# Two graph layers on one core: how the list matrices are compared, how the largest entries are taken, and where the last packing and the ranking stand

## The chip, the cores and the metric

The kernel runs on one core of one Trainium2 chip. The metric is the device time of one execution in microseconds (us), as the median over runs. The profile is one further execution, recorded by the hardware profiler; its times are counted from the start of its span. TensorE is PE in the profile, VectorE is DVE, ScalarE is ACT, GpSimd is POOL and SyncE, which issues plain DMAs, is SP.

## The reference

There are N = 2708 nodes with D = 512 features and a sparse matrix `adj` of 2708 x 2708 with about eight entries besides the diagonal in a row. Two layers follow each other, each with a residual and a layer norm:

```
# layer 0
d  = rowsum(adj) ** -0.5
x1 = layernorm(x + relu((d[:,None] * adj * d[None,:]) @ x @ W + b))
# layer 1, H = 4 heads
z     = x1 @ W_node + b_node
feats = z @ K[h]                               # per head
attn  = softmax(s_i + NEG * (1 - adj))         # NEG = -1e10
out   = layernorm(x1 + relu(mean_h(attn @ feats)))
```

With NEG = -1e10 the softmax of a row puts all its weight on the row's largest entry of `adj`, as long as the second is far enough below it. So layer 1 is computed as `u = x1 @ M + c`, with M and c made from `W_node`, `b_node` and the mean of `K`, and each node then takes the row of `u` that its largest entry points at. Rows where two entries are too near set a value in `bad`; if any is set, a dense version of the whole runs behind the fast one.

## The kernel before

Rows are worked in 21 full blocks of 128 (`ib` 0 to 20) and a last one of 20 rows, 22 blocks in all (`NB`), in an order written out by hand: nothing is reordered by a scheduler, each engine has its own queue, and a queue runs in program order.

**Setup stage, to about 139 us.** Each block of `adj` is loaded (1354 KB), the diagonal is taken out by POOL, ACT sums the rows (L299), and `v = d * (x @ W)` goes to memory as `v_d`. DVE searches each block in three column ranges: eight largest values and their places, `vals` and `ats` (L318, L319). The searches of the last blocks run on into the main stage, two or three for each block.

**Main stage, 139 to about 428 us.** A block's product with the sparse matrix is a sum of nine chunks (`CHUNKS`, c = 0 to 8). In each third of the columns one chunk ("d") takes every row's first entry, and two ("l") take the other entries as a list of 128 slots each. For every chunk POOL issues an indirect DMA that gathers 128 rows of `v_d` (L611, one per chunk, nine per block). PE multiplies the gathered rows by a small matrix `s` (L672), or DVE scales and adds them for some "d" chunks (L662). The order is by chunk: in chunk n = 9 * ib + c the program first issues the gathers up to chunk n + 11 (later up to n + 22, by two more for each block), so POOL's queue holds gathers that lie ahead of what PE consumes.

The lists are made by `hot` (DVE, L392 and L393: a matrix with a one for each pair of slot and row), `enlist` (PE, L402: this matrix times the packed entries of the block) and `listed` (DVE, L414 to L439). `hot` of block ib + 3 stands at chunk 5 of block ib, `enlist` four chunks later, `listed` six. `pack_1`, `pack_2`, `pack_3` bring the search's results into the packed form, for the blocks in `GROUPS` 0-3, 4-11 and 12-21; the last group is packed when the search has ended.

At the end of a block DVE adds the block's own row (`own_term`, L698 or L700; bias by PE where `bias_on_pe`), takes relu and residual (`norm_1`, L711, L712), ACT squares (L727 or L721), and the inverse root comes from POOL (L733, in `norm_2`, up to block 9) or from ACT and DVE (`root_1`, `root_2`). ACT writes the norm (`norm_3`, L756), PE turns it at chunk 7 of the next block (L224), and `u_product` (L235) makes `u` of a block one block later, at chunk 5. PE waits in its queue for each of these.

**The rank steps.** Some rows (more than eight entries in a third, or lists over 256; and the 20 rows of the last block) can't be done by lists. They are marked in `flag`, counted and collected as one extra block of up to 128 rows, called L. `largest` finds each row's largest entry among its three thirds and its diagonal; `rank_1`, `rank_1b`, `rank_2` count and number the marked rows and those whose largest entry points at a late block; `rank_3` builds one-hot matrices (`l_hot`, L923); `rank_3b` multiplies on PE; `rank_4` turns the sheet into row numbers. Then `listed_a` makes POOL gather the 128 marked rows of `adj` itself (`l_a`, L983) and of x (`l_x`). ACT sums `l_a` (`listed_sum`, L989), POOL takes its root (`listed_root`), and PE multiplies `l_a` by all of v: 22 times `listed_turn` (a transposition, L1003) and `listed_product` (L1012), fed by loads `l_v` on SP. After the last one `listed_norm` (L1019) finishes block L.

The places of these steps are in `plan`, whose keys are (blocks after the search ended, chunk). The search ends in block 7, so `found_at` is 8 and (0, 5) is chunk 5 of block 8. `listed_turn` runs at the odd chunks from chunk 4 of block 11 on, `listed_product` at the even ones, two behind.

**Last stage.** Once `u` of the first 18 blocks and of block L is in memory, POOL gathers for every node the row of `u` that it needs (L1052), DVE and ACT finish the second norm, and the results are stored; rows that were marked are scattered by indirect DMAs (L1029).

Of the kernel before, what the change touches and what calls it, by code (L numbers as in the profile page):

```python
# [47 lines left out]
P = 128  # L48
# [15 lines left out]
def tile_two_graph_layers(  # L64
# [60 lines left out]
    nc.gpsimd.memset(half_neg, -0.5)  # L125
    ones = const.tile([P, 1], F32, name="ones")
# [66 lines left out]
    nc.gpsimd.iota(own_row, pattern=[[P, NB]], base=0, channel_multiplier=1, **small_numbers)  # L193
    for t in range(T):
        nc.gpsimd.memset(third[:, t, :], float(CUT[t]))
# [50 lines left out]
    def pieces(dst, left):  # L246

        piece = wpool.tile([T, D], BF16, name="piece_3", bufs=1)
        for k in range(T):
            nc.vector.tensor_copy(piece, left)  # L250
            if k == 0:
                nc.vector.tensor_scalar(dst, piece, ident[:T, 0:1], None, op0=ALU.mult)
            else:
                nc.vector.scalar_tensor_tensor(dst, piece, ident[:T, k : k + 1], dst, op0=ALU.mult, op1=ALU.add)
            if k < T - 1:
                nc.vector.tensor_sub(left, left, piece)
# [128 lines left out]
    def hot(ib):  # L385

        lo = max(g for g in GROUPS if g <= ib)
        ends = starts[lo]
        h_t = search.tile([P, T, 2 * P], BF16, name="hot", bufs=2)
        for t in range(T):  # L390
            past = search.tile([P, 2 * P], BF16, name="past", bufs=2)
            nc.vector.tensor_scalar(past, slots, ends[:, 1, ib - lo, t : t + 1], None, op0=ALU.is_gt)  # L392
            nc.vector.scalar_tensor_tensor(  # L393
                h_t[:, t, :], slots, ends[:, 0, ib - lo, t : t + 1], past, op0=ALU.is_gt, op1=ALU.subtract
            )
        hots[ib] = h_t

    def enlist(ib):
        ls = sheets[ib] = p_one.tile([P, D], F32, name="ls")
        h_t = hots.pop(ib)  # L400
        for k in range(NL):
            nc.tensor.matmul(  # L402
                ls[:, k * W_REC : (k + 1) * W_REC],
                h_t[:, k // 2, k % 2 * P : (k % 2 + 1) * P],
                packed[:, ib, k // 2, :],
                start=True,
                stop=True,
            )

    def listed(ib):  # L410
# [5 lines left out]
        nc.vector.tensor_copy(minus_row, ls[:, :, 0])  # L416
# [36 lines left out]
    def group(lo):  # L453
# [4 lines left out]
        if hi == NB:  # L458
            nc.vector.memset(flag[: N - full, NS:], 1.0)
# [228 lines left out]
    def bias_on_pe(ib):  # L688

        return ib < 9  # L690

    def own_term(ib):
# [3 lines left out]
        if bias_on_pe(ib):  # L696
            if ib in BY_VECTOR:
                nc.vector.tensor_scalar(vs[:pr], vs[:pr], self_d[:pr, ib : ib + 1], None, op0=ALU.mult)  # L698
# [122 lines left out]
    def largest():  # L821

        best, nxt, sel, lower, dif = (col() for _ in range(5))
        j = dl["j"] = search.tile([P, NB], F32, name="largest")
        nc.vector.tensor_copy(best, vals[:, :, 0, 0])
        nc.vector.tensor_copy(nxt, vals[:, :, 0, 1])
        nc.vector.tensor_copy(j, cols[:, :, 0, 0])
        for t in range(1, T + 1):
            other = vals[:, :, t, 0] if t < T else aii
            at_t = cols[:, :, t, 0] if t < T else own_row  # L830
            nc.vector.tensor_tensor(sel, other, best, op=ALU.is_gt)
            nc.vector.tensor_tensor(lower, other, best, op=ALU.min)
            nc.vector.tensor_max(nxt, nxt, lower)
            if t < T:
                nc.vector.tensor_max(nxt, nxt, vals[:, :, t, 1])
            nc.vector.tensor_max(best, best, other)
            nc.vector.tensor_tensor(dif, at_t, j, op=ALU.subtract)
            nc.vector.tensor_mul(dif, dif, sel)
            nc.vector.tensor_add(j, j, dif)
        nc.vector.tensor_copy(idx, j)  # L840
        nc.vector.tensor_scalar(best, best, 1.0, -NEG, op0=ALU.subtract, op1=ALU.mult)
# [605 lines left out]
```

## Time and profile before

| | |
|---|---|
| Median of 14 runs | 489.35 us (486.18 to 491.05) |
| Profiled execution | 488.0 us, its span 486.3 us |
| Instructions in the span | 5318 |
| PE busy | 374.9 us, 1129 matmuls |
| DVE busy | 391.9 us, 1079 instructions |
| ACT busy | 312.5 us |
| POOL busy | 307.3 us |
| Mean granted PE clock | 0.92 |
| DMA traffic | 140.67 MB, mean 289 GB/s |

The profiled execution's own time is 1.7 us above its span and 1.35 us below the median of the runs. A block's end is the end of its L712 on DVE: block 7 ends at 252.3 us, block 8 at 271.3, block 9 at 284.8, block 10 at 298.2, block 11 at 314.0, block 12 at 326.1, block 16 at 378.7 and block 20 at 428.0 us. A busy PE is not PE at its peak, since ends of matmuls are modelled; the distance from one start to the next is the better measure.

### The profile page before, as it was taken

The numbers are of one execution on the slowest core, as the hardware profiler recorded it, in microseconds if no ns is written. First come the engines' busy times: TensorE is split into PE (matmuls) and PEld (weight loads), VectorE is DVE, ScalarE is ACT, GpSimd is POOL, SyncE is SP. The second block draws the span as 40 slices with busy tenths as digits, with TensorE's granted clock in tenths as the row PEclk, the third lists the DMA queues.
The fourth block names the chain that finished last, engine by engine and source line by source line (L and its number), as shares of the span: only waits on it lengthen the run. The fifth ranks groups of instructions, "written<-read, shape, count | busy, mean of one in ns | idle before, by whom it ended". The sixth has DMA issues, their size and how long they took to land.

```text
span 486.3 us, 5318 instructions
## 1 busy us (share of the span) xinstructions
PE 374.9 (77%) x1129; PEld 167.9 (35%) x1129; DVE 391.9 (81%) x1079; ACT 312.5 (64%) x575; POOL 307.3 (63%) x434
## 2 busy tenths in 40 slices
PE   4978787687987989799979859699999999870000
PEld 3434343333223333343433324344444344340000
DVE  2899989889699999999999997676666797567661
ACT  1599999897985556776773453865566322348780
POOL 2343544454477677777877677777777665677713
PEclk9999999898998989899998959899999999996555
DMA  7999999999538678889889789999999788468962
GB/s 223 423 394 415 425 341 373 350 339 350 195 113 292 190 235 265 268 249 310 271 259 297 225 264 358 388 335 387 356 363 316 231 272 269 126 191 293 326 212 84
DMA packets 51565, 140.67 MB, mean 289 GB/s; under 512 B 10617, under 2 KB 10617, under 8 KB 48688
## 3 DMA queue, kind: packets, MB, share of 16 engines
q0 software_dynamic: 21840, 68.29, 45.3%
q1 hardware_dynamic: 29684, 71.95, 39.3%
q14 instruction: 30, 0.25, 0.2%
q8 instruction: 11, 0.18, 0.2%
HBM read 117.33 MB, written 24.99 MB: 293 GB/s over the span
## 4 chain that ended last, share of the span: by engine, by line
DVE 31%; DMA 29%; PE 21%; issue 8%; POOL 5%; ACT 4%; SPq 1%; POOLq 0%; DVEq 0%; ACTq 0%
DMA a<-in_adj_dram 18%; PE acc L672 8%; DVE ats L319 6%; PE po L235 6%; DVE vals L318 5%; PE acc_l L1012 4%; DMA g<-u_e,idx 3%; DVE hot L393 3%; DMA x<-in_x_dram 3%; DVE vs L662 2%; DMA l_a<-in_adj_dram,to_read 2%; POOL g L611 2%; PE po L504 1%; DVE past L392 1%; DVE h_early L712 1%
## 5 line engine op out<-in xcount | busy, mean ns | idle before, releaser
L611 POOL DMA_INDIRECT g<-v_d,l_col x126 | 128.1, 1016 | 40.4 <-issue 22.4
L672 PE MATMUL acc<-g,s 128*128 128x512 f32 x278 | 144.7, 634 | 4.9 <-DMA g<-v_d,l_col 3.0
L235 PE MATMUL po<-m_sb,sT 128*128 128x512 f32 x176 | 81.0, 604 | 4.0 <-ACT sT L226 4.0
L235 PE MATMUL acc<-w_sb,sT 128*128 128x512 f32 (+1 forms) x176 | 84.1, 623 | 0.0
L611 POOL DMA_INDIRECT g<-v_d,cols x63 | 63.8, 1012 | 19.8 <-issue 11.6
L318 DVE MAX8 vals<-a 128x8 f32<-128x896 f32 (+2 forms) x66 | 71.7, 1086 | 2.0 <-ACT a L299 2.0
L319 DVE FIND_INDEX8 ats<-vals,a 128x8 uint32<-128x896 f32 (+2 forms) x66 | 72.0, 1091 | 0.0
L672 PEld LDWEIGHTS acc<-g,s 128*128 128x128 f32 x278 | 50.3, 201 | 50.1 <-issue 42.0
L305 ACT ACTIVATE a<-a 128x2708 f32<-128x2708 f32 (+1 forms) x22 | 54.1, 2460 | 13.6 <-DVE ats L319 13.6
L299 ACT ACTIVATE a<-a 128x2708 f32<-128x2708 f32 (+1 forms) x22 | 54.5, 2475 | 10.0 <-POOL a L311 9.8
L235 PEld LDWEIGHTS po<-m_sb,sT 128*128 128x128 f32 x176 | 33.5, 194 | 46.5 <-issue 38.5
L235 PEld LDWEIGHTS acc<-w_sb,sT 128*128 128x128 f32 (+1 forms) x176 | 32.9, 198 | 35.2 <-issue 35.2
L649 ACT ACTIVATE s<-s,l_val,l_minus 128x128 f32<-128x128 f32 x86 | 42.4, 493 | 2.9
L311 POOL TENSOR_SCALAR_AFFINE_SELECT a<-a 128x128 f32<-128x128 f32 (+1 forms) x22 | 7.0, 320 | 56.7 <-DMA a<-in_adj_dram 49.2
L226 ACT COPY sT<-tp 128x512 f32<-128x512 f32 (+1 forms) x44 | 25.5, 579 | 26.6 <-PE tp L224 26.6
L662 DVE SCALAR_TENSOR_TENSOR vs<-g,scaled,vs 128x512 f32<-128x512 f32 x50 | 37.3, 745 | 0.1
L224 PE MATMUL tp<-ident,x 128*128 128x128 f32 (+1 forms) x88 | 15.1, 298 | 28.7 <-DMA x<-in_x_dram 18.8
L648 ACT ACTIVATE s<-place,l_row 128x128 f32<-128x128 f32 x86 | 33.4, 388 | 0.0
L393 DVE SCALAR_TENSOR_TENSOR hot<-slots,ends,past 128x256 bf16<-128x256 bf16 x63 | 30.6, 485 | 2.2
L1052 POOL DMA_INDIRECT g<-u_e,idx x21 | 22.9, 1091 | 7.4 <-issue 5.5
L224 PEld LDWEIGHTS tp<-ident,x 128*128 128x128 f32 (+1 forms) x88 | 10.3, 151 | 40.6 <-issue 23.5
L721 ACT ACTIVATE xr<-h_late,nms 128x512 f32<-128x512 f32 x11 | 7.9, 722 | 24.9 <-DVE nms L720 24.9
(265 smaller groups left out, 570.5 us busy)
## 6 DMA issues: line engine op xcount, KB each, us to landing
a<-in_adj_dram SPq DMA_DIRECT2D x21, 1354.0 KB, 15.2
x<-in_x_dram SPq DMA_DIRECT2D x21, 256.0 KB, 14.3
vs<-v_d SPq DMA_DIRECT2D x21, 256.0 KB, 4.5
xr<-in_x_dram SPq DMA_DIRECT2D x21, 256.0 KB, 6.4
l_v<-v_d SPq DMA_DIRECT2D x21, 256.0 KB, 5.5
u_e<-ut SPq DMA_DIRECT2D x17, 256.0 KB, 4.2
h_d<-h_late SPq DMA_DIRECT2D x13, 256.0 KB, 3.9
out_dram<-h_late SPq DMA_DIRECT2D x13, 256.0 KB, 3.9
```

Of the source, the lines that this page charges most:

```text
L226: copy(sT[:, :, :pr], ps[:, :, :pr])
L235: nc.tensor.matmul(po[:pr], sT[:, f, :pr], wt[:, f, :], start=(f == 0 and row_3 is None), stop=(f == ND - 1))
L299: nc.scalar.activation(a, a, AF.Copy, accum_out=sums[:pr, ib : ib + 1])
L305: nc.scalar.activation(a, a, AF.Relu, scale=-1.0, accum_out=bad[:pr, NB + ib : NB + ib + 1])
L318: nc.vector.max(out=vals[:pr, ib, t, :], in_=part)
L319: nc.vector.max_index(out=ats[:pr, ib, t, :], in_max=vals[:pr, ib, t, :], in_values=part)
L393: nc.vector.scalar_tensor_tensor(h_t[:, t, :], slots, ends[:, 0, ib - lo, t : t + 1], past, op0=ALU.is_gt, op1=ALU.subtract)
L611: nc.gpsimd.indirect_dma_start(out=t[:pr], out_offset=None, in_=src, in_offset=bass.IndirectOffsetOnAxis(ap=ap, axis=0))
L648: nc.scalar.activation(s[:, :pr], place[:, :pr], AF.Abs, bias=minus_row[:, t : t + 1])
L649: nc.scalar.activation(s[:, :pr], s[:, :pr], AF.Relu, scale=minus_val[:, t : t + 1], bias=val[:, t : t + 1])
L662: nc.vector.scalar_tensor_tensor(vs, g, scaled[:, ib, CHUNKS[c][1], 0:1], vs, op0=ALU.mult, op1=ALU.add)
L672: nc.tensor.matmul(acc[ib][:pr], ss.pop((ib, c))[:k, :pr], g[:k], start=(first and not bias_on_pe(ib)), stop=(c == len(CHUNKS) - 1),)
```

## The change

- `hot` writes two comparisons for each third, one with the starts and one with the ends times -1, instead of a comparison and a combined second one; `enlist` adds the two on PE (twelve matmuls in place of six).
- The copy of `minus_row` and, for blocks 1 to 11, `own_term` go from DVE to ACT; `bias_on_pe` holds for twelve blocks instead of nine.
- `pieces` takes the three bf16 parts of a bias row with `below` in fewer steps.
- `largest` compares four candidates (three thirds and the diagonal) at once with reductions, in three steps; the third has some ten small operations (the second largest, ties, `bad`). Before, it was three copies, three rounds of seven or eight small operations, and six more.
- The last group's packing and the rank steps stand at more places of `plan`, from chunk 2 of block 8 to chunk 5 of block 12, where they stood from chunk 2 of block 8 to chunk 3 of block 10. `rank_2` and `rank_4` are cut up.
- The root of the row sums of the marked rows comes as three more columns of `told` through `rank_3b` (from `dinv`, which is known), so `listed_sum` and `listed_root` are gone.
- `listed_a` stands at chunk 3 of block 12 (it was at chunk 6 of block 10); `listed_turn` starts at chunk 3 of block 13 and runs in two of three chunks, and `listed_product` may run in the same chunk as a `listed_turn`.
- `hot` is no longer left out in the block after the search has ended.

```diff
@@ pieces
-        for k in range(T):
+        for k in range(1, T):
             nc.vector.tensor_copy(piece, left)
-            if k == 0:
-                nc.vector.tensor_scalar(dst, piece, ident[:T, 0:1], None, op0=ALU.mult)
-            else:
-                nc.vector.scalar_tensor_tensor(dst, piece, ident[:T, k : k + 1], dst, op0=ALU.mult, op1=ALU.add)
-            if k < T - 1:
-                nc.vector.tensor_sub(left, left, piece)
+            nc.vector.scalar_tensor_tensor(left, piece, below[:, k - 1 : k], left, op0=ALU.mult, op1=ALU.add)
+        nc.vector.tensor_copy(dst, left)
@@ hot
-        h_t = search.tile([P, T, 2 * P], BF16, name="hot", bufs=2)
+        h_t = search.tile([P, T, 2, 2 * P], BF16, name="hot", bufs=2)
         for t in range(T):
-            past = search.tile([P, 2 * P], BF16, name="past", bufs=2)
-            nc.vector.tensor_scalar(past, slots, ends[:, 1, ib - lo, t : t + 1], None, op0=ALU.is_gt)
-            nc.vector.scalar_tensor_tensor(
-                h_t[:, t, :], slots, ends[:, 0, ib - lo, t : t + 1], past, op0=ALU.is_gt, op1=ALU.subtract
+            nc.vector.tensor_scalar(h_t[:, t, 0], slots, ends[:, 0, ib - lo, t : t + 1], None, op0=ALU.is_gt)
+            nc.vector.tensor_scalar(
+                h_t[:, t, 1], slots, ends[:, 1, ib - lo, t : t + 1], -1.0, op0=ALU.is_gt, op1=ALU.mult
             )
@@ enlist
         for k in range(NL):
...
+            for i in range(2):
+                nc.tensor.matmul(
+                    ls[:, k * W_REC : (k + 1) * W_REC],
+                    h_t[:, k // 2, i, k % 2 * P : (k % 2 + 1) * P],
+                    packed[:, ib, k // 2, :],
+                    start=(i == 0),
+                    stop=(i == 1),
+                )
@@ listed
-        nc.vector.tensor_copy(minus_row, ls[:, :, 0])
+        nc.scalar.copy(minus_row, ls[:, :, 0])
@@ group
-        if hi == NB:
-            nc.vector.memset(flag[: N - full, NS:], 1.0)
+    def last_group():
+        pack_3(GROUPS[2], NB)
+        nc.vector.memset(flag[: N - full, NS:], 1.0)
@@ bias_on_pe, own_term
-        return ib < 9
+        return ib < 12
...
-                nc.vector.tensor_scalar(vs[:pr], vs[:pr], self_d[:pr, ib : ib + 1], None, op0=ALU.mult)
+                nc.scalar.activation(vs[:pr], vs[:pr], AF.Copy, scale=self_d[:pr, ib : ib + 1])
@@ largest, largest_2, largest_3
+        nc.vector.tensor_copy(tops[:, :, :T], vals[:, :, :, 0])
+        nc.vector.tensor_copy(tops[:, :, T], aii)
+        nc.vector.tensor_copy(at[:, :, :T], cols[:, :, :, 0])
+        nc.vector.tensor_copy(at[:, :, T], own_row)
+        nc.vector.tensor_reduce(nxt, vals[:, :, :, 1], axis=AX.X, op=ALU.max)
+        nc.vector.tensor_reduce(best, tops, axis=AX.X, op=ALU.max)
+    def largest_2():
+        nc.vector.tensor_tensor(is_top, tops, best.unsqueeze(2).to_broadcast([P, NB, T + 1]), op=ALU.is_equal)
+        nc.vector.tensor_mul(at, at, is_top)
+        nc.vector.tensor_reduce(j, at, axis=AX.X, op=ALU.max)
         nc.vector.tensor_copy(idx, j)
+    def largest_3():
...
@@ rank_2 is cut into rank_2, rank_2b, rank_2c; in rank_2c:
+        d_3 = late.tile([P, NB, 3], BF16, name="d_3")
...
+        nc.vector.tensor_tensor(
+            told[:, :, n_told:], d_3, dl["kind"][:, 0, :].unsqueeze(2).to_broadcast([P, NB, 3]), op=ALU.mult
+        )
@@ rank_4 (first five operations) and rank_5 (the rest)
+        nc.vector.tensor_reduce(dl["d"], dl["ls"][:, K * 5 : K * 5 + 3], axis=AX.X, op=ALU.add)
@@ listed_sum and listed_root are removed
-        nc.scalar.activation(dl["a"], dl["a"], AF.Copy, accum_out=s2)
-        root(dl["d"], dl["s2"])
@@ plan
-        (0, 5): [largest],
-        (0, 8): [rank_1],
-        (1, 3): [rank_1b],
-        (1, 4): [rank_2],
-        (1, 6): [rank_3],
-        (2, 2): [rank_3b],
-        (2, 3): [rank_4],
-        (2, 6): [lambda: listed_a(), lambda: [listed_v(jb) for jb in range(6)]],
-        (3, 2): [listed_sum],
-        (3, 8): [listed_root],
+        (0, 4): [lambda: pack_2(GROUPS[2], NB)],
+        (0, 7): [last_group],
+        (1, 1): [largest],
+        (1, 4): [largest_2],
+        (1, 7): [largest_3],
+        (2, 0): [rank_1],
+        (2, 3): [rank_1b],
+        (2, 4): [rank_2],
+        (2, 7): [rank_2b],
+        (3, 0): [rank_2c],
+        (3, 2): [lambda: rank_3(0)],
+        (3, 5): [lambda: rank_3(1)],
+        (3, 8): [rank_3b],
+        (4, 1): [rank_4],
+        (4, 3): [lambda: listed_a(), lambda: [listed_v(jb) for jb in range(6)]],
+        (4, 5): [rank_5],
@@ the main loop
-                and not (c == 5 and found_at is not None and ib == found_at + 1)
...
-                group(GROUPS[2])
+                pack_1(GROUPS[2], NB)
...
-            if found_at == ib - 3 and c == 4:
+            if found_at == ib - 5 and c == 3:
                 products_l = list(range(NB))
-            if c % 2 and products_l:
+            if c % 3 != 2 and products_l:
                 listed_turn(products_l.pop(0))
-            elif len(dl.get("turned", [])) > (2 if products_l else 0):
+            if len(dl.get("turned", [])) > (2 if products_l else 0):
                 listed_product(dl["turned"].pop(0))
```

## The prediction

> **What bounds the kernel now.** I read the page's totals first, then its main stage as a table of windows, one for each block:
>
> ```profile
> PE 374.9 (77%) x1129; PEld 167.9 (35%) x1129; DVE 391.9 (81%) x1079; ACT 312.5 (64%) x575; POOL 307.3 (63%) x434
> ...
> ```
>
> ```profile
> core 0: us, PE busy (x) PEld busy (x) DVE busy (x) ACT busy (x) POOL busy (x), PEclk, DMA share, GB/s
> 240.60:252.30 11.70, 11.16 (x35) 4.25 (x33) 11.35 (x31) 8.30 (x17) 9.36 (x10) 1.00 0.82 261
> 252.30:271.30 19.00, 14.04 (x40) 6.34 (x41) 17.78 (x90) 7.68 (x20) 13.48 (x15) 0.91 0.86 272
> 271.30:284.80 13.50, 11.06 (x47) 4.68 (x45) 12.85 (x44) 5.83 (x15) 9.51 (x10) 0.90 0.74 213
> 284.80:298.20 13.40, 10.40 (x34) 4.96 (x35) 11.95 (x47) 7.52 (x19) 10.18 (x11) 0.72 0.99 332
> 298.20:314.00 15.80, 11.76 (x35) 5.02 (x34) 8.96 (x30) 11.55 (x23) 11.69 (x15) 0.89 1.02 393
> 314.00:326.10 12.10, 12.10 (x41) 5.64 (x40) 9.04 (x30) 8.17 (x22) 9.36 (x10) 1.00 0.95 337
> 326.10:339.30 13.20, 13.20 (x44) 6.22 (x43) 9.02 (x30) 8.17 (x22) 10.15 (x11) 1.00 1.02 372
> ```
>
> Rows one to seven are blocks 7 to 13. In block 8 DVE is full for 17.8 of 19.0 us: that is the packing and ranking. In blocks 12 and 13 PE is full. By these rows the burst on DVE costs blocks 8 to 11 61.7 us where four blocks like block 7 take 46.8, and a reader would stop at a gain of 15 us. The next view, POOL in order of time, says why not (busy 80% a block, but each gather is followed by 0.30 us in which its queue takes the next):
>
> ```profile
> 268.68 0.95 POOL L611 DMA_INDIRECT g<-v_d,cols  x1 [0.30 <-issue]
> 272.67 0.57 POOL L733 TENSOR_TENSOR rss<-sqs,half_neg 128x1 f32<-128x1 f32 x1 [3.04 <-ACT sqs L728]
> 273.43 0.99 POOL L611 DMA_INDIRECT g<-v_d,l_col  x1 [0.18 <-issue]
> ...
> 292.61 0.95 POOL L611 DMA_INDIRECT l_a<-in_adj_dram,to_read  x1 [0.30 <-issue]
> ...
> 318.96 1.20 POOL L611 DMA_INDIRECT g<-v_d,cols  x1 [0.30 <-DMA g<-v_d,l_col]
> ```
>
> From 168 to 320 us POOL has one long wait, the 3.04 us shown; otherwise it goes from gather to gather, 1.25 us each. POOL is the hidden bound up to the gather of `l_a`. What hangs on that gather is in the chain of waits, and PE in order of time shows the rest:
>
> ```profile
> 292.61 10.12 DMA l_a<-in_adj_dram,to_read
> 302.75 2.55 ACT l_a L989 x2
> 305.32 1.28 ACT L742
> ```
>
> ```profile
> 328.30 0.27 PE L1003 MATMUL po<-ident,l_a 128*128 128x128 f32 x1
> ...
> 421.96 1.88 PE L672 MATMUL acc<-g,s 128*128 128x512 f32 x4
> ```
>
> PE waits for `l_a` (first turn at 305.35), and then has almost no gap until its last chunk ends at 421.96 + 1.88 = 423.84. So the end is set by: POOL's queue up to `l_a`, its landing, the PE work behind it, and 62.5 us of last stage (486.3 - 423.8), which moves with it.
>
> **The change, part by part.** *Lists.* Six operations of `hot` take 198.30 to 200.46 = 2.16 us of DVE:
>
> ```profile
> 198.30 0.28 DVE L392 TENSOR_SCALAR past<-slots,ends 128x256 bf16<-128x256 bf16 x1
> 198.62 0.49 DVE L393 SCALAR_TENSOR_TENSOR hot<-slots,ends,past 128x256 bf16<-128x256 bf16 x1
> ```
>
> ```profile
> 198.65 0.96 POOL L611 DMA_INDIRECT g<-v_d,cols  x1 [0.30 <-issue]
> ```
>
> Six independent ones like L392, about 0.21 from start to start, take 1.3: DVE gains 0.9 per block. PE pays six more small matmuls in `enlist`; six now take 0.15 us from start to start, so +0.15 per block. Two operations more of the L392 kind lie over POOL's gathers; the gather at 198.65, inside the six, took 0.96, as outside, so I charge nothing (bounds: 0, and 0.3 per block if each compare held one gather for its own 0.28).
>
> The Trainium skill's page "SBUF — State Buffer", section "SBUF: two separate sides", speaks against this part: a DVE operation with one source in its two-port mode locks GpSimd out of the port through which it writes a gather's descriptors. By that rule three more such compares per block cost POOL up to 3 x 0.28 = 0.84 us a block, an estimate from that page, 9 us by block 13, and the change would lose. The row at 198.65 does not show it.
>
> *To ACT.* `own_term` leaves DVE (L698, 8 x 0.50 us; L700, three of 0.74) for ACT at about 0.69 (L540, the same shape), and the copy of `minus_row` (0.16) too. ACT is busy 8 of 12 us, and the operand was loaded a block ahead: nothing, or 0.7 us a block where ACT is late. The bias of blocks 9 to 11 costs PE 3 x 0.32. All this lies before `l_a`, where POOL sets the pace. `pieces` saves DVE some 1.6 us at 133 us; block 0 then waits for gathers instead, so 0.4 at its end.
>
> *Packing and ranking spread.* Block 8 now carries 4.9 (pack, 253.8 to 258.7) + 5.05 (largest, 261.5 to 266.6) + 0.9 us on DVE beyond a normal block, block 9 4.5 + 3.1, block 10 2.8. After it: block 8 about 10 us of DVE, block 9 10, block 10 11, block 11 13.5 (rank_2c 2.3, l_hot 3.1, three vector chunks 2.0, lists 2.6, norm and own 2.1, the rest 1.4), block 12 11. No block but 11 exceeds POOL's nine gathers (11.3 us, 12 with the root of L733). Up to block 10 the root stays in POOL's queue between gathers, and ACT and PE's turn at chunk 7 need it: PE cannot run ahead of POOL there. So DVE's relief is paid out only as POOL's removed waits. Block 8 should end near 263, block 10 near 286, block 12 near 310.
>
> *Waits added.* `enlist` of block 14, at chunk 0 of block 12, needs the PSUM buffer `ls` that `rank_4` reads one chunk later: PE stands until DVE has closed block 11 and read it (1.4 for L711 and L712, 0.7 for a chunk, 0.3: 2.4 us; in block 10 the same wait took 3.4), with the chunks of block 12 behind it. It lies before PE's wait for `l_a`, which takes it up; without that cover it costs all of it. ACT's copy of `minus_row` waits for `enlist`, with small matrices queued behind it that PE needs 11 chunks later: nothing.
>
> *POOL up to `l_a`.* At chunk 3 of block 12 gathers are issued up to chunk n + 13, that is to (13, 6), the gather at 318.96. It ends with its gap at 320.46. Removed in front: `l_a` and `l_x` themselves (292.61 to 295.12, 2.51; they now come behind), the root of the marked rows (2.07, from 310.26 to 312.33), the wait at 272.67 (3.02), two small ones (1.13), 0.4 of block 0. So `l_a` is issued at 320.46 - 9.1 = 311.3, not 292.6: 18.7 us later.
>
> *Landing.* 10.1 us before, with six `l_v` loads (1.5 MB) in flight; now SP issues those some 8 us ahead. At the bytes of that stretch (3.8 MB, 1.2 of them `l_v`) I take 10.1 x (1 - 1.2/3.8) = 7.0. Bounds: 6.4 (an `adj` load in the chain, 122.23) and 15.2 (the median of the `adj` loads on a full DMA). So PE resumes at 318.3; it reaches chunk 3 of block 13 near 312.5, a wait of 6 us. What the wait hides is everything before it.
>
> *PE behind it.* Before, from the turn at (13, 3), 328.30, to the end: 95.5. By then 7 turns and 5 products were done that are now still to do: 7 x 0.11 + 5 x 0.86 = 5.1. Five lists: 0.75. The wait lets the clock drop: block 11, whose wait is alike, was granted 0.89 of 15.8, so 1.7 (bounds 0 and 1.7). Minus 1.2, since the last product comes one chunk earlier and `hot` of block 20 is shorter, two waits of 0.68 and 0.50 at 389 to 391. Sum 101.9; end at 420.2, against 423.84: 3.6 us gained. Turns and products in blocks 14 to 16 make these blocks 13.1 + 2 x 0.97 + 0.15 = 15.2 us.
>
> The skill's page "TensorE: Matmul & The Clock Gate", section "What's actually happening", has the clock at half after an idle window of about 3.4 us and until one of activity has passed. The rows agree (0.72 and 0.89 in blocks 10 and 11, after waits of 3.4 and 2.4 us), and by the rule alone the drop costs 1.7 us too.
>
> *Last stage.* It starts from u of block 17 and of L, which PE makes: it moves with PE. Sum: 488.0 - 3.6 = 484.4 for the profiled execution, which stood 1.35 below the median: **485.7 us**.
>
> **The rivals.** *Late row (slower).* If `l_a` lands later than 10.6 us after its issue (311.3 + 10.6 = 321.9), the postponed listing loses. At 15.2 it lands at 326.5: +4.6, 493.9. For it: DMA shares of 0.95 to 1.02 from block 10 on. Against: SP has little to load while PE waits.
>
> *Full relief (much faster).* If POOL's queue shortens with DVE's load, so that `l_a` lands when PE gets to block 13 (312.5), there is no wait and no drop: 312.5 + 100.2 = 412.7, a gain of 11.1, 478.2. Against: gaps of 0.30 that no wait explains.
>
> *Nothing gained.* Landing as before (10.1): end at 311.3 + 10.1 + 101.9 = 423.3, gain 0.5, 488.8.
>
> **How the numbers follow.** Forecast 0.52, with its own range 482.5 to 488 (landing 6.4 to 9, POOL 2 us either way); nothing gained 0.16; late row, with POOL held by the compares to the same effect, 0.20; full relief 0.12. Runs differ by about 0.3% (1.5 us), about what a measurement of this kernel can tell from no change. Faster: 0.12 + 0.49 of the forecast = 0.61; same 0.16 + 0.03 = 0.19; slower 0.20. The range reaches into both ends: 479 to 491.5.
>
> **What would show it.** Right: `l_a` issued at 309 to 313 and PE idle 4 to 8 us before its first turn; blocks 8 to 10 of 11 to 12.5 us; POOL without its 3 us wait; blocks 14 to 16 of 15.2 us with PE full; 62.5 us behind PE's last chunk. Wrong: `l_a` issued before 307, gathers above 1.1 us on average, PE with gaps in blocks 14 to 16 (then `l_v` or `l_t` is late), or an end that does not follow PE.

## The result, and the profile after

The changed kernel takes **503.2 us** (median of 10 runs, 499.65 to 508.65) against 490.0 us for the kernel before (47 runs, 486.18 to 493.06): a ratio of 1.0266, 95% interval 1.024 to 1.0293. The forecast was 485.7 us, with 479 to 491.5 as its range and 0.20 for slower: so the change is slower where a gain was forecast, and the time lies outside the range. The profiled execution took 500.51 us, its span 498.7 us.

The page's totals of the changed kernel:

```profile
PE 379.7 (76%) x1258; PEld 171.9 (34%) x1258; DVE 364.1 (73%) x1036; ACT 317.7 (64%) x605; POOL 301.2 (60%) x434
```

DVE has 27.8 us less to do than before and POOL 6.1 us less; PE has 4.8 us more, ACT 5.2. Nothing here says slower. The windows of the main stage, one row for each of blocks 7 to 14 of the changed kernel (us; busy time and instructions of each engine; granted PE clock; DMA share; GB/s):

```profile
core 0: us, PE busy (x) PEld busy (x) DVE busy (x) ACT busy (x) POOL busy (x), PEclk, DMA share, GB/s
247.20:258.00 10.80, 9.85 (x38) 4.12 (x37) 9.99 (x29) 7.86 (x17) 8.30 (x9) 1.00 0.86 278
258.00:276.70 18.70, 11.27 (x37) 5.22 (x38) 11.07 (x48) 9.26 (x25) 12.40 (x13) 0.73 0.83 261
276.70:288.70 12.00, 12.00 (x43) 5.38 (x43) 9.57 (x45) 6.62 (x17) 8.24 (x9) 1.00 0.73 228
288.70:300.60 11.90, 11.26 (x43) 5.21 (x41) 9.55 (x46) 8.20 (x21) 9.28 (x11) 1.00 0.88 293
300.60:314.30 13.70, 8.15 (x41) 3.61 (x39) 13.11 (x42) 8.85 (x20) 10.95 (x10) 0.85 0.83 276
314.30:328.80 14.50, 13.44 (x51) 6.43 (x52) 10.79 (x46) 7.46 (x19) 11.02 (x12) 0.79 0.99 356
328.80:344.80 16.00, 12.09 (x46) 5.44 (x45) 8.18 (x29) 8.22 (x23) 11.96 (x13) 1.00 1.03 404
344.80:361.10 16.30, 15.45 (x55) 7.11 (x54) 8.03 (x27) 8.55 (x25) 12.27 (x13) 1.00 1.00 371
```

DVE's load did fall as forecast (block 8: 11.07 us, before 17.78), and yet block 8 still takes 18.7 us, with no engine full in it: all of them wait. Block 11 ends 0.3 us after before's. Blocks 12 to 16 then take 79.4 us where before takes 64.7, but most of that is the listing of block L, which now stands there: the kernel without the wait (below, "behind `own_f`") takes 79.2 us for the same five blocks, 5.3 of them in PE's wait for `l_a`. Against that kernel, which ends block 8 at 258.0 us, this one is 18.7 us behind at the end of block 8 and 16.4 at the end of block 11. The view of waits names a pair that the view of before does not have at all (engine, tile and line, what it waited for: us in total, times, longest):

```profile
DVE own_f L438 <- ACT l_row L428: 42.1, 19, 5.6
...
PE po L251 <- ACT l_t L1057: 5.7, 4, 3.1
```

DVE in order of time, and ACT beside it, show one of the 19 (start, us, what; in brackets the idle time before it and who ended it):

```profile
184.14 0.14 DVE L426 TENSOR_TENSOR nth<-slot_no,ls 128x6 f32<-128x6 f32 x1
184.32 0.20 DVE L430 TENSOR_TENSOR one<-count,nth 128x36 f32<-128x36 f32 x1
187.45 0.34 DVE L438 TENSOR_TENSOR own_f<-ls,one 128x180 f32<-128x180 f32 x1 [2.94 <-ACT l_row L428]
```

```profile
184.84 2.44 ACT L317 ACTIVATE a<-a 128x2708 f32<-128x2708 f32 x1
...
187.28 0.14 ACT L428 COPY l_row<-ls 128x6 f32<-128x6 f32 x1
```

`nth`, the copy into `minus_row` (the tile `l_row`) and `own_f` all read the sheet `ls` in PSUM. `own_f` needs nothing that the copy writes, but the waits show that the program keeps reads of this tile by different engines in the order in which they are written: ACT's copy waits for DVE's `nth` (twice, 1.1 us in all), DVE's `own_f` for ACT's copy (19 times, 42.1 us). The copy takes 0.14 us. It stands in ACT's queue behind whatever was issued before it, here a pass of 2.44 us over a block of `adj`, and DVE stands for 2.94 us. Before, all three were on DVE, and its own queue kept the order.

The Trainium skill's page "PSUM — Partial Sum Buffer", section "PSUM bank collisions raise a hardware error", says why such an order is written: two engines must not touch the same bank in the same partitions at once, two readers (ScalarE beside VectorE) included, and software has to order them. The wait of 2.94 us is what this order costs here; the collision itself no run here shows.

What the delay of DVE reaches is seen in DVE, POOL and PE in order of time, and behind POOL in its row of the view of waits:

```profile
263.35 0.35 DVE L438 TENSOR_TENSOR own_f<-ls,one 128x180 f32<-128x180 f32 x1 [5.01 <-ACT l_row L428]
...
265.19 0.18 DVE L344 TENSOR_SCALAR cb<-cnt 128x30 bf16<-128x30 f32 x1
```

```profile
278.13 0.56 POOL L747 TENSOR_TENSOR rss<-sqs,half_neg 128x1 f32<-128x1 f32 x1 [3.67 <-ACT sqs L742]
...
320.11 0.95 POOL L625 DMA_INDIRECT l_a<-in_adj_dram,to_read  x1 [0.31 <-DVE hot L404]
```

```profile
POOL rss L747 <- ACT sqs L742: 11.2, 6, 3.7
```

```profile
265.43 0.21 PE L346 MATMUL po<-cb,before 128*128 128x30 bf16 x1 [8.38 <-DVE cb L344]
...
330.23 0.33 PE L1055 MATMUL po<-ident,l_a 128*128 128x128 f32 x1 [0.77 <-DMA l_a<-in_adj_dram,to_read]
...
351.83 3.70 PE L251 MATMUL po<-m_sb,sT 128*128 128x512 f32 x8 [0.85 <-ACT l_t L1057]
...
435.61 1.88 PE L686 MATMUL acc<-g,s 128*128 128x512 f32 x4
```

DVE late makes the norm late, ACT squares late, and POOL, which takes the root in its queue between gathers, stands for 3.67 us, and for 11.2 us in six such waits. So gathers and `l_a` are late: issued at 320.11, forecast 311.3. Packing (`cb`) stands behind an `own_f` that waits 5.01 us, and PE, which needs `cb`, stands 8.38 us in block 8. From block 13 on the row `nbs` of the norm is late (in block 14 it waits 1.64 us for DVE, until 350.48), `l_t` stands behind the norm in ACT's queue (351.53), and PE waits for it. PE's last chunk ends at 437.49, before 423.84: 13.7 us later. The last stage takes 61.2 us (before 62.5), which leaves 12.4 us in the span.

### The profile page after: what moved, and what is told of

It reads as the page before. It is cut to its first block, busy times and chain, and to the rows that moved or that the text cites. A ratio compares the mean times of both kernels' runs of the same rounds, so it can differ in the third digit from the quotient of the medians.

```text
span 498.7 us, 5582 instructions
## 1 busy us (share of the span) xinstructions
PE 379.7 (76%) x1258; PEld 171.9 (34%) x1258; DVE 364.1 (73%) x1036; ACT 317.7 (64%) x605; POOL 301.2 (60%) x434
## 3 DMA queue, kind: packets, MB, share of 16 engines
q1 hardware_dynamic: 29684, 71.95, 38.5%
## 5 line engine op out<-in xcount | busy, mean ns | idle before, releaser
L625 POOL DMA_INDIRECT g<-v_d,l_col x126 | 124.1, 985 | 53.7 <-issue 24.2
L251 PE MATMUL acc<-w_sb,sT 128*128 128x512 f32 (+1 forms) x176 | 85.4, 631 | 0.0
L625 POOL DMA_INDIRECT g<-v_d,cols x63 | 65.1, 1033 | 19.7 <-issue 12.8
L686 PEld LDWEIGHTS acc<-g,s 128*128 128x128 f32 x278 | 51.4, 199 | 57.8 <-issue 48.8
L438 DVE TENSOR_TENSOR own_f<-ls,one 128x180 f32<-128x180 f32 x21 | 7.3, 345 | 42.3 <-ACT l_row L428 42.1
L1104 POOL DMA_INDIRECT g<-u_e,idx x21 | 21.7, 1032 | 7.7 <-issue 4.9
L804 DVE TENSOR_TENSOR ut<-po,c_bc 128x512 f32<-128x512 f32 x15 | 10.3, 688 | 21.7 <-PE po L251 21.7
```

The lines of the kernel that those rows point to most:

```text
L251: nc.tensor.matmul(po[:pr], sT[:, f, :pr], wt[:, f, :], start=(f == 0 and row_3 is None), stop=(f == ND - 1))
L625: nc.gpsimd.indirect_dma_start(out=t[:pr], out_offset=None, in_=src, in_offset=bass.IndirectOffsetOnAxis(ap=ap, axis=0))
L686: nc.tensor.matmul(acc[ib][:pr], ss.pop((ib, c))[:k, :pr], g[:k], start=(first and not bias_on_pe(ib)), stop=(c == len(CHUNKS) - 1),)
L1104: nc.gpsimd.indirect_dma_start(out=t, out_offset=None, in_=src, in_offset=bass.IndirectOffsetOnAxis(ap=at, axis=0), bounds_check=n - 1, oo ...
```

## The experiments

Ratios are to the kernel before, run on the same chip in the same group. The first eight runs fell in two groups in which the kernel before takes 536.3 and 532.6 us. Why these were slower is not shown: in their traces much of the idle time has no releaser that the profile can name, and chip 11, which gave 536.3 us, gave 489.4 us later. So only their ratios are used, and the decisive kernels were run again in groups in which before takes 489.4 to 490.1 us; times in us below are from these.

**Theories.** *Reads of `ls`*: the copy on ACT makes DVE wait, and that is the loss. *Places*: the late place of `l_a` and the turns after it lose. *Compares*: the additional operations on DVE hold POOL's gathers or PE's lists.

**The copy alone, taken out and put in.** On the changed kernel, and the reverse on the kernel before:

```diff
-        nc.scalar.copy(minus_row, ls[:, :, 0])
+        nc.vector.tensor_copy(minus_row, ls[:, :, 0])
```

> The changed kernel with one edit: the copy of minus_row is on DVE again. Theory (the wait of DVE for ACT): in the changed kernel own_f on DVE waits for ACT's l_row 19 times, 42.1 us in all, and what stands behind it on DVE makes the losses of blocks 1 to 7 (5.7 us) and of the products of block L (PE waits 0.85 us a block for l_t, 3.14 in block 13). Without it: waits of own_f under 2 us in all, block 7 ends at 249 to 252 us (after: 258.0), block 8 at 262 to 267 (276.7), PE without the 0.85 us waits in blocks 14 to 17, time 483 to 491 us (after 503, before 490). Rival (the postponed listing costs the time): blocks 1 to 8 recover 5 us, but the 22 products still lie late, and the time is 496 to 500 us. Rival (two compares hold POOL or PE): 499 to 503 us.

> The kernel before with one edit of the change: the copy of minus_row on ACT, all else as it was. Theory (the wait of DVE for ACT): DVE is the fuller engine here (11.35 us of 11.7 a block in blocks 4 to 7), so a wait of 2 to 3 us in each block adds to it nearly whole: blocks 1 to 7 slower by 8 to 16 us in all, own_f waiting over 30 us in all, time 498 to 510 us (before 490). Rival (the copy costs what it takes on ACT, 0.14 us a block; the loss of the change lies elsewhere): 489 to 492 us.

Ratios 1.0035 (0.9993 to 1.0077) without the copy on ACT, 1.0347 (1.0254 to 1.0439) for before with it. The changed kernel unaltered and the first of these, in a second group:

> The changed kernel as it is, beside the kernels without its wait, on one chip: the yardstick for them. Every theory expects 1.024 to 1.03 of before, as measured.

> The changed kernel with the copy of minus_row on DVE, a second time, since the transfers of the first chip landed late and hid what a few us would show. Theory (the wait of DVE for ACT is the whole loss): 0.99 to 1.004 of before; where transfers land as in the profile of before, the time is 483 to 491 us, block 8 ends at 262 to 267 us, l_a is issued 309 to 315. Rival (a part of the loss is the postponed listing): 1.008 to 1.02.

1.0226 (1.0105 to 1.0347) and 1.01 (1.0035 to 1.0165). In these groups, then, the change without the copy on ACT is level with before or 1% slower, against 2.3% with it; the last two intervals meet, so these times alone don't settle it. The traces show the wait itself gone: `own_f` waits for `l_row` 13 times, 28.4 us, in the unaltered kernel, and never without the copy on ACT. Before with the copy alone, in a group where the times can be compared:

> The kernel before with the copy of minus_row on ACT alone, a second time. Theory (the wait of DVE for ACT): 12 to 20 us slower than before, 502 to 510 us, own_f waiting for l_row over 30 us in all, block 7 ending at 259 to 266 us (before 252.3). Rival (the first value, 1.035, came from late transfers): under 497 us.

511.79 us, 1.046 (1.0407 to 1.0512), a little above what was expected: one instruction of 0.14 us moved between engines costs 22.4 us, and its view of waits has the same pair, with the same 2.94 us as one instance of it in DVE's order of time:

```profile
DVE own_f L426 <- ACT l_row L416: 38.5, 18, 4.0
```

```profile
190.01 0.35 DVE L426 TENSOR_TENSOR own_f<-ls,one 128x180 f32<-128x180 f32 x1 [2.94 <-ACT l_row L416]
```

**The copy on ACT, but behind `own_f`.** It then waits for DVE, and nobody on DVE waits for it:

```diff
-        nc.scalar.copy(minus_row, ls[:, :, 0])
...
         nc.vector.tensor_tensor(own_f, ...)
+        nc.scalar.copy(minus_row, ls[:, :, 0])
```

> The changed kernel with the copy of minus_row still on ACT, but written three operations later, behind own_f: ACT now waits for DVE, and no operation of DVE waits for it. Theory (the wait, not the place of the copy): within 2 us of the kernel with the copy on DVE, 483 to 492 us, no wait of own_f for l_row. Rival (ACT has no room for the copy, and the small matrices behind it come late): 498 to 504 us as the changed kernel, with PE waiting for small matrices.

> The changed kernel with the copy of minus_row on ACT behind own_f, a second time, for its profile and its time beside the next kernels. Theory (the wait of DVE for ACT is the whole loss): 0.99 to 1.003 of before, own_f without a wait for l_row; where transfers land as in the profile of before, block 8 ends at 262 to 267 us and PE does not wait for l_t in blocks 14 to 17. Rival (a part of the loss is the postponed listing): 1.006 to 1.015.

First 0.9996 (0.9955 to 1.0038), then **484.49 us, 0.9883 (0.9855 to 0.9911)**. The same edit list with its lines in another order is 18.7 us faster than the change (503.2 - 484.49; 15.2 between the two profiled executions), and 5.6 us faster than before, a little more than was expected. DVE and ACT in order of time:

```profile
177.16 0.26 DVE L429 TENSOR_TENSOR one<-count,nth 128x36 f32<-128x36 f32 x1
177.45 0.35 DVE L437 TENSOR_TENSOR own_f<-ls,one 128x180 f32<-128x180 f32 x1
```

```profile
177.68 2.44 ACT L317 ACTIVATE a<-a 128x2708 f32<-128x2708 f32 x1
180.12 0.14 ACT L443 COPY l_row<-ls 128x6 f32<-128x6 f32 x1
```

The copy is still behind the pass of 2.44 us, and DVE is not held by it. The order is now the other way round: ACT waits three times for `own_f`, 2.8 us in all, and PE once for the copy, 0.8 us. Its POOL (in order of time, and its row of the view of waits) and PE show the prediction's steps:

```profile
307.95 0.95 POOL L625 DMA_INDIRECT l_a<-in_adj_dram,to_read  x1 [0.30 <-issue]
```

```profile
POOL rss L747 <- ACT sqs L742: 1.9, 1, 1.9
```

```profile
248.29 0.19 PE L346 MATMUL po<-cb,before 128*128 128x30 bf16 x1 [0.71 <-DVE cb L344]
...
317.65 0.47 PE L1055 MATMUL po<-ident,l_a 128*128 128x128 f32 x1 [5.27 <-DMA l_a<-in_adj_dram,to_read]
```

The wait for `cb` is 0.71 us, not 8.38. POOL's waits for the squares are 1.9 us, not 11.2, which is 9.3 of the 12.2 us by which `l_a` is issued earlier. Of the 16.4 us that the changed kernel lies behind at the end of block 11, PE's wait for `l_a` takes up a part (5.27 us here, 0.77 there), and PE's waits for `l_t` put as much back: 16.6 us at PE's last chunk (437.49 and 420.88). *Reads of `ls`* holds.

**Where in the kernel it costs.** The copy on ACT (in its old line) in blocks below 12 only, and from 12 on only, on DVE in the others:

```diff
-        nc.scalar.copy(minus_row, ls[:, :, 0])
+        if ib < 12:    # the other kernel: ib >= 12
+            nc.scalar.copy(minus_row, ls[:, :, 0])
+        else:
+            nc.vector.tensor_copy(minus_row, ls[:, :, 0])
```

> The changed kernel with the copy of minus_row on ACT for the lists of blocks 0 to 11 alone (made up to block 8, while ACT also has the passes of 2.44 us over adj), on DVE for the others. Theory: the profile of the changed kernel stood 5.4 us behind before at the end of block 8, so 5 to 8 us of the 13 are lost here: 1.008 to 1.016 of before. Rival (the loss comes from the blocks with the products of L alone): as without the wait, 0.995 to 1.004.

> The changed kernel with the copy of minus_row on ACT for the lists of blocks 12 to 20 alone (made from block 9 on), on DVE for the others. Theory: waits of 1.6 to 2 us of own_f make DVE's root late, ACT's norm with it, and PE waits for l_t behind that norm, 3.1 us in block 13 and 0.85 in each of blocks 14 to 17: 5 to 8 us, 1.008 to 1.016 of before. Rival (PE is full from block 12 on and covers it): 0.995 to 1.004.

495.19 us (1.0116, 1.0087 to 1.0145) and 487.71 us (0.9948, 0.9918 to 0.9979). The second expectation, 5 to 8 us lost and 1.008 to 1.016, failed: the loss is 3.2 us. From the views of waits of the first and the second, and PE in order of time of the second:

```profile
DVE own_f L441 <- ACT l_row L429: 31.5, 12, 5.5
```

```profile
DVE own_f L441 <- ACT l_row L429: 10.2, 7, 1.9
```

```profile
356.23 3.70 PE L251 MATMUL po<-m_sb,sT 128*128 128x512 f32 x8 [0.85 <-ACT l_t L1060]
```

Over the 484.49 of the copy behind `own_f`, the first lists cost 10.7 us and the last 3.2: 13.9 of the 18.7, the rest only with both. A wait of 31.5 us costs 10.7 and one of 10.2 costs 3.2: about a third of what DVE stands ends in the time. With both it is more, 18.7 of 42.1 us, and 22.4 of 38.5 in the kernel before. The row of 0.85 us is the same as in the changed kernel: late lists delay `l_t`.

**The two compares alone**, on the kernel before (`hot` and `enlist` of the diff in the front):

> The kernel before with the list matrices alone changed: two compares for each third, twelve matmuls in enlist. The prediction's step: DVE 0.9 us a block less, PE 0.15 more, POOL's gathers as before, so next to nothing up to block 11 where POOL sets the pace, and 0.15 us a block for PE behind it: 488 to 491 us (before 490). Rival (the compares lock POOL out of its port, up to 0.84 us a block): gathers of 1.05 us or more on average between 210 and 252 us (before 1.02), time 493 to 500 us. Rival (DVE sets the pace in blocks 1 to 11): 482 to 487 us.

> The kernel before with the two compares and the twelve matmuls alone, a second time, since the first interval (0.997 to 1.006) held both answers. Theory (DVE sets the pace in blocks 0 to 4, where it also searches): 0.9 us in each of five blocks reaches l_a and the end: 484.5 to 487.5 us (before 490). Rival (the prediction: POOL sets the pace up to l_a): 489 to 491 us.

First 1.0017 (0.9971 to 1.0064), then 484.48 us, 0.9897 (0.9863 to 0.993): 5.5 us faster, where the prediction gave this part next to nothing. Its windows for blocks 3 and 4, which take 11.7 us each before, with DVE 11.35 busy:

```profile
190.30:201.00 10.70, 9.32 (x36) 4.04 (x36) 10.46 (x29) 9.06 (x19) 8.67 (x9) 1.00 0.85 270
201.00:211.70 10.70, 10.70 (x40) 4.55 (x39) 10.46 (x29) 7.56 (x15) 8.37 (x10) 1.00 0.86 283
```

And POOL in order of time, where the root waits 1.84 and 0.46 us (before 3.10 and 3.04):

```profile
166.55 0.57 POOL L733 TENSOR_TENSOR rss<-sqs,half_neg 128x1 f32<-128x1 f32 x1 [1.84 <-ACT sqs L728]
...
267.89 0.57 POOL L733 TENSOR_TENSOR rss<-sqs,half_neg 128x1 f32<-128x1 f32 x1 [0.46 <-ACT sqs L728]
```

`l_a` is issued at 287.9 us, before at 292.61: 4.7 earlier, 3.8 of it from these two waits. PE's last chunk ends at 421.29, 2.6 us earlier; how the rest of the 5.5 us comes was not followed. *Compares* falls.

**`own_term` on ACT.** Put back to DVE on the changed kernel with the copy on DVE, and, as in this diff, put alone on the kernel before:

```diff
-        return ib < 9
+        return ib < 12
...
-                nc.vector.tensor_scalar(vs[:pr], vs[:pr], self_d[:pr, ib : ib + 1], None, op0=ALU.mult)
+                nc.scalar.activation(vs[:pr], vs[:pr], AF.Copy, scale=self_d[:pr, ib : ib + 1])
```

> The changed kernel with the copy of minus_row on DVE, and with own_term of blocks 1 to 8 back on DVE and of blocks 9 to 11 too (no bias by PE there): the other step that went to ACT is undone. The prediction's step (to ACT: nothing, or 0.7 us a block where ACT is late): within 1.5 us of the kernel with own_term on ACT. Rival (DVE sets the pace in blocks 1 to 11, so its relief of 0.5 us a block was a gain): 3 to 5 us slower. Rival (ACT is late for the norm of the block and its own_term stands in the way): 2 to 6 us faster.

> The kernel before with own_term of blocks 1 to 11 on ACT (bias by PE up to block 11) and nothing else. Theory (DVE sets the pace in blocks 0 to 4): 0.4 to 0.5 us in each of four or five blocks, 487 to 489 us. Rival (the prediction: nothing, or 0.7 us a block where ACT is late): 489.5 to 495 us.

The first, 1.0029 (0.9955 to 1.0104), decides nothing. The second takes 485.18 us, 0.9899 (0.9876 to 0.9923): 4.8 us faster, more than either side of its expectation. Both parts together, the compares and `own_term`:

> The kernel before with the two compares and with own_term on ACT (bias by PE up to block 11), nothing else. If the two gains add up (both are DVE's time in blocks 0 to 4): 479.5 to 480.5 us (before 490), and the rest of the change, which the kernel at 481.6 us also holds, brings nothing or costs. If PE or POOL takes over as the bound once DVE has one of them: 481 to 484 us.

483.23 us, 0.9851 (0.9795 to 0.9907): 6.2 us by the medians, 7.3 by the ratio, where the two gains add up to 10.3. Whether they add up stays open: the product of the two ratios, 0.9797, lies just inside the interval, and in the profiled executions PE's last chunk ends 2.6 us earlier with the first part (421.29), 1.7 with the second (422.15) and 4.8 with both (419.06, before 423.84).

**The old places.** The changed kernel with the copy on DVE, and packing, ranking, `listed_a` and the turns where the kernel before has them:

```diff
 plan:
+        (0, 5): [largest, largest_2, largest_3],  (0, 8): [rank_1],
+        (1, 4): [rank_2, rank_2b, rank_2c],  (1, 6): [both halves of rank_3],
+        (2, 3): [rank_4, rank_5],  (2, 6): [listed_a, listed_v],
-            if found_at == ib - 5 and c == 3:
+            if found_at == ib - 3 and c == 4:
```

> The changed kernel with the copy of minus_row on DVE, and with the packing, the ranking, the gather of l_a and the products of block L at the places and in the cadence of before (the steps of largest and of rank_2 one behind the other, hot left out in the block after the search); lists, own_term and the root without ACT stay changed. The prediction's step: the spread takes waits from POOL and moves the products behind, for a net gain of 3 to 4 us, so this kernel is 3 to 4 us slower than the one with the new places. Rival (the postponed listing leaves PE idle before l_a and piles the products up behind): this kernel is 3 to 6 us faster than the one with the new places. Rival (PE has the same work behind either way): within 1.5 us.

> The changed kernel with the copy on DVE and the rank steps and the products of L at the places of before, a second time, beside the kernel with the new places. The prediction's step: 3 to 4 us slower than it. Rival (the postponed listing costs): 3 to 6 us faster than it. Rival (PE has the same work behind either way): within 1.5 us of it.

First 1.002 (0.9973 to 1.0066), then 481.6 us, 0.982 (0.9792 to 0.9849): 2.9 us faster than 484.49, with intervals that do not meet. So *Places* is right in sign, for a sixth of the size of the loss. Sums over the windows of PE from block 7's end to its last chunk, of the copy behind `own_f` and of the old places:

```profile
sum 175.60, PE 158.08 PEld 71.89 DVE 120.31 ACT 89.03 POOL 124.11; mean PE 15.81 PEld 7.19 DVE 12.03 ACT 8.90 POOL 12.41
```

```profile
sum 169.90, PE 158.10 PEld 71.77 DVE 121.25 ACT 87.91 POOL 125.14; mean PE 15.81 PEld 7.18 DVE 12.12 ACT 8.79 POOL 12.51
```

PE does the same work (158.1 us) and stands 5.7 us more with the new places; 2.5 of this is the longer wait for `l_a` (5.27 against 2.74 us).

**Turns later.** If the wait for `l_a` is what remains, starting the turns a few chunks later takes it up, in either arrangement: from chunk 7 instead of 4 of block 11 (old places), and from chunk 7 instead of 3 of block 13 (new places, copy behind `own_f`).

```diff
-            if found_at == ib - 3 and c == 4:
+            if found_at == ib - 3 and c == 7:
```

```diff
-            if found_at == ib - 5 and c == 3:
+            if found_at == ib - 5 and c == 7:
```

> The changed kernel with the copy on DVE and the rank steps at the places of before (481.6 us), with the turns of l_a begun three chunks later, at chunk 7 of block 11. Theory (PE's idle time before l_a is a cost): the wait of 2.74 us and the slower clock behind it (0.91 of 18.1 us, 1.6 us) go, PE does three chunks of block 11 meanwhile: 478 to 480.5 us. Rival (the products end three chunks later and the last stage with them): 481 to 484 us.

> The changed kernel with the copy on ACT behind own_f and the new places (484.5 us), with the turns of l_a begun four chunks later, at chunk 7 of block 13. Theory (what the new places cost is PE's idle time before l_a): the wait of 5.27 us and the slower clock behind it (0.83 of 19.9 us) go: 478.5 to 481 us, level with the old places. Rival (the new places cost by the products piled up behind): 483.5 to 486 us.

With the old places **479.87 us, 0.9788 (0.9753 to 0.9822)**, the fastest version here, 10.1 us below the kernel before; PE waits 0.86 us for `l_a`. The 1.7 us to the version without this edit are not clear of noise, as the two intervals meet. With the new places 488.41 us, 0.9956 (0.9924 to 0.9988), 3.9 us slower than without the edit: this expectation failed. DVE, ACT and PE of it in order of time:

```profile
325.50 0.75 DVE L714 SCALAR_TENSOR_TENSOR vs<-vs,self_d,b_bc 128x512 f32<-128x512 f32 x1 [6.42 <-DMA vs<-v_d]
```

```profile
327.81 0.72 ACT L735 ACTIVATE xr<-h_late,nms 128x512 f32<-128x512 f32 x1 [6.08 <-DVE nms L734]
```

```profile
329.64 0.47 PE L1055 MATMUL po<-ident,l_a 128*128 128x128 f32 x1 [4.33 <-ACT l_t L1057]
```

PE no longer waits for `l_a`, but the load of a block's own row, `vs`, issued at 312.58 us while `l_a` is under way, lands 12.89 us later (the median of these loads in the copy-behind kernel is 5.4), with the DMA's share at 1.01 to 1.03. DVE waits 6.42 us for it, ACT for DVE, and PE waits 4.33 us for `l_t`. The wait has moved, from one transfer in a full DMA to the next.

## Why the prediction was wrong, and where it was right

**The step that failed** is the second of "Waits added": "ACT's copy of `minus_row` waits for `enlist`, with small matrices queued behind it that PE needs 11 chunks later: nothing." It asked what is queued behind the moved instruction on its new engine. It did not ask who, on the old engine, comes after it in the order of reads of `ls`. The copy was costed at 0.16 us of DVE saved; it cost 18.7 us in the changed kernel and 22.4 us alone. The first of "Waits added", PE's wait for the buffer `ls`, came as described, 3.1 us in the changed kernel and 3.8 with the copy behind `own_f`, forecast 2.4. None of the rivals held the second; the price of "late row", 493.9, was reached by another way and passed.

**The forecast's sum, term by term.** The kernel with the copy behind `own_f` is the change without that wait, and the terms can be compared:

| term | forecast | changed kernel | copy behind `own_f` |
|---|---|---|---|
| `l_a` issued | 311.3 | 320.11 | 307.95 |
| landing, to PE's first turn | 7.0 | 10.12 | 9.70 |
| PE behind it | 101.9 | 107.26 | 103.23 |
| PE's last chunk ends | 420.2 | 437.49 | 420.88 |
| last stage | 62.5 | 61.2 | 62.7 |
| profiled execution | 484.4 | 500.51 | 485.31 |

- *POOL up to `l_a`*: 8.8 us later than forecast in the changed kernel, through the waits of POOL's root; without them 3.35 us earlier. PE stands 0.77 us before its first turn in the changed kernel and 5.27 us without the waits, where 4 to 8 was the sign.
- *Landing*: mis-sized in both. Forecast 7.0 since `l_v` was to be out of the way; it took 10.12 and 9.70, as before (10.1), although in the copy-behind kernel `l_v` was issued 8 us ahead of `l_a`, as forecast (299.89 and 307.95). So scaling the landing by the bytes in flight did not hold; what sets it is open. In the copy-behind kernel this offsets the earlier issue, so the agreement of 420.2 and 420.88 is partly two errors that cancel.
- *PE behind it*: 5.4 us over in the changed kernel, where PE's waits for `l_t` are 5.7 us, a sign the prediction had named ("PE with gaps in blocks 14 to 16 (then `l_v` or `l_t` is late)"); 1.3 over without them. Blocks 14 to 16 of 15.2 us with PE full came there, as this window of block 14 of the copy-behind kernel shows (block 15 is alike); in the changed kernel they are 16.3 us:

```profile
331.60:346.70 15.10, 15.10 (x55) 7.18 (x54) 8.17 (x27) 8.56 (x25) 11.45 (x13) 1.00 0.98 362
```

- *Last stage* moves with PE: right for the kernels of the table (61.2 to 62.7); in other kernels here it is 59.8 (turns later, new places) to 64.5 us (old places).
- *Packing and ranking spread*: the forecast had this as the source of its 3.6 us. Block 8 was to end near 263 and ended at 258.0 without the wait (276.7 with it); but the new places cost 2.9 us against the old ones.
- *Lists* and *To ACT*: costed at about nothing, they bring 5.5 and 4.8 us alone, 6.2 to 7.3 together. The prediction showed block 7 with DVE 11.35 busy of 11.70 and took POOL for the bound; taking DVE's load away shortened blocks 3 and 4 by 1.0 us each. What it said of POOL was half right: 3.8 of 4.7 us came as POOL's removed waits, but the one at 166 us, which it had not counted, gave 1.3 of them.
- *Nothing gained*, *full relief*: neither came. The landing that *nothing gained* assumed did come (10.1), beside an earlier issue of `l_a`.

So without the wait the forecast stood 0.9 us from the profiled execution (484.4 and 485.31), and part of that agreement is luck: an earlier issue of `l_a` from parts priced at nothing, against a longer landing.

**Open.** Why the new places cost 2.9 us beyond the wait for `l_a` is not settled (2.5 of PE's 5.7 us are explained; the two kernels also differ in the engine of the copy). Whether the gains of the compares and of `own_term` add up is open too. What `largest`, `pieces` and the root of the marked rows bring alone was not tried. `own_term` back on DVE in the changed kernel stays undecided.

## What to carry to other kernels

When an instruction that reads a PSUM tile is moved to another engine, look at the reads of the same tile that stay behind it: here they waited for it, through the whole in-order queue of the new engine, and a copy of 0.14 us held the old engine for up to 5.6 us a time. Put the moved read last, so that only the slack engine waits. And look at the next transfer before starting the user of a late one later: with the DMA full, the new places lost 3.9 us by it, where the old places lost nothing.

## What the runs showed of the hardware that was not expected

The comparison with one source, as the change uses it, did not hold the gathers: from 210 to 252 us a gather took 0.989 us on average with the two compares alone and 1.022 before (1.048 in the first run of the same kernel, in the slower group, where there is no profile of before). Over the main stage, of the gathers that lay over the old combined operation (L393, two sources), 29% took over 1.1 us, of those over the new comparisons 3% (changed kernel, compares alone) to 6% (copy behind `own_f`), of those over neither 11 to 17%. The Trainium skill's page "SBUF — State Buffer", section "SBUF: two separate sides", by which the prediction had feared the new form, has a one-source operation in a two-port mode shut the gathers out; whether these comparisons run in that mode no view shows, and 3 to 6% is no sign of it. The section names operations with two sources too, against GpSimd work that reads SBUF, which would go with the 29%, though 17% over neither in the same kernel leaves little of it, and with the halves of `l_hot` below; whether a gather reads SBUF in this sense no run here tests.

The halves of `l_hot` (two sources, 1.61 us each on DVE) did hold gathers. A gather that began under a half ended 0.81 to 0.83 us after it: in the changed kernel the halves end at 306.93 and 311.04, the gathers under them at 307.75 (2.21 us long) and 311.87 (1.23 us), and with the copy behind `own_f` the first of the two took 2.15 us. With the old places, where the halves follow each other at once, one gather was held over both, for 3.43 us. Before has the same halves, also at once, but there a gather began 0.4 us before the end of each, took 1.24 and 1.23 us, and the first was not held by the second half.
